# Sharing a group's scores between VectorE and GpSimd, and the order of halvings, folds and row sums in it

## The chip, the cores and the metric

The kernel runs on one core of a Trainium2 chip. The metric is the time of one execution in device microseconds; lower is better. A core has TensorE (PE in the profile), VectorE (DVE), ScalarE (ACT), GpSimd (POOL) and SyncE (SP), each with an in-order queue of instructions of its own, and DMA queues that SyncE and GpSimd issue to.

## The reference

The input x is 8 batches of 512 tokens of 256 numbers. Four blocks follow each other, each adding its result to x: attention A, a feed-forward block, attention B, the same feed-forward block.

```python
x = x + attn_a(layernorm(x))
x = x + ffn(layernorm(x))
x = x + attn_b(layernorm(x))
x = x + ffn(layernorm(x))
# attn_a: 16 heads of 64 channels; it attends over the channels of one token
scores = einsum('bshq,bshk->bshqk', Q / 8, K)     # one 64 x 64 matrix per token and head
w = softmax(where(k > q, -inf, scores))
attn = einsum('bshqk,bshk->bshq', w, V) @ Wo + bo
# ffn
h = silu(x @ w1) * (x @ w2)      # 1024 hidden; w1, w2, h1, h2, w3 ternary with scales
h = gelu(h @ h1); h = gelu(h @ h2); return h @ w3
# attn_b: ordinary causal attention over the 512 tokens, 16 heads of 16
```

Attention A has no matrix product in its middle: each token has its own 64 x 64 causal matrix of products q[i] k[j] for each head, whose exponentials are summed, and summed once more weighted with v[j].

## The kernel before, in words

**Attention A** works in groups: 128 tokens on the partitions and 4 heads, so 8 batches x 4 head groups x 4 token tiles = 128 groups. A causal triangle of 64 is cut into squares: for n = 32, 16, 8, 4, 2, 1 there are 64 / (2n) squares of n x n for a head, and the diagonal is kept by itself. A group's squares make four *units*: unit 0 the 32-squares of two heads, unit 1 all 16-squares, unit 2 the 32-squares of the other two heads, unit 3 all the small ones (8, 4, 2, 1). Units 0, 1 and 2 each have a work tile of 4096 numbers a partition, made in two pieces of 1024: one half of each block of columns for the exponentials (the denominator), the other for the exponentials times v (the numerator). Tiles of units 0 and 2 share a ring of three buffers, unit 1 has one buffer ("w16"), unit 3 one ("ws").

Each unit passes through these operations:

- `scores` (L784): products of q and k, two pieces. Units 0 and 2 on GpSimd, units 1 and 3 on VectorE.
- `exps` (L798): the exponential, on ScalarE.
- `weigh` (L808): times v, on VectorE.
- `halve` (L814): an accumulating DMA, issued from GpSimd's queue, adds one half of the tile to the other (1,024 KB).
- `fold` (L819), units 0 and 2 alone: a further halving, an addition on GpSimd.
- `gather` (L845): VectorE sums the rows of what is left; a row sum for each square size goes into a small tile `red`.
- `add_rows` (L852): GpSimd adds the row sums to `acc`, which holds numerator and denominator of the group. `small_squares` does so for n = 2 and 1 (one addition at L835, two at L852).
- `invert` (L856, VectorE's reciprocal) and `divide` (L860, GpSimd) finish the group; then TensorE turns it over and multiplies with Wo.

**The order is written out by hand.** `AttentionA.step(n)` emits, for step n, the operations of several units at different stages (a software pipeline): the scores of unit n, the exponentials of unit n - 1, weigh and halve of unit n - 2, and so on; four steps make a group. A step has three parts, with a `yield` after each. The instruction queue of each engine holds its instructions in just the order in which `step` emits them, so an instruction that has to wait holds up all that stands behind it on that engine.

**The other blocks** (feed-forward, attention B, feed-forward of the batch before) are a second generator, `after_a`. After each part of a step the driver takes from it as much as is due: every `yield` of `after_a` gives a cost in us, their sum over a batch is `total` (309.5), and this sum is spread evenly over the 64 steps of a batch. The blocks of batch b start 11 steps after the last step of attention A of that batch, so attention A of batch 0 runs by itself and the blocks of batch 7 run by themselves at the end. Work in these blocks is put off with `later` and emitted at the next `flush`.

**The gate of a feed-forward block**: h = silu(p1) * p2 is kept as a high part in a rounded 32-bit format for TensorE and the remainder h - high (L1036, GpSimd), so that two products give the precision of one. The tiles p1 and p2 (128 x 512 each) come from a ring of five PSUM buffers, `ps_f`.

**At the start**, `fit_qkv` prepares the attention weights of one head group (on VectorE for group 0, on GpSimd for groups 1 to 3, with two DMA loads of bias rows and two stores to DRAM on SyncE's queue), and the generator `later_weights` (`prep`) prepares those of the other blocks. `measure` takes mean and variance of a batch's tokens.

Of the kernel before, what the change touches and what calls it, by code (L numbers as in the profile page):

```python
# [26 lines left out]
GW = GH * C  # L27
NG = HID // GW
# [256 lines left out]
def fast_path(ctx: ExitStack, tc: tile.TileContext, k, t, flag):  # L285

    nc = tc.nc
# [182 lines left out]
    def plus(ps, xi):  # L470

        nc.tensor.matmul(ps, ident, xi, start=False, stop=True)

    rends = const.tile([P, 2, NB], F32, name="rends")
    means = const.tile([P, NB, 2, NT], F32, name="means")

# [127 lines left out]
    class AttentionA:  # L604
# [32 lines left out]

        def step(self, n):

            weighed = self.at(n - 2)  # L640
            if weighed[0] is not None:
                self.weigh(*weighed)
            unit = self.at(n)
            on_pool = unit[3] in (0, 2)
            if on_pool:
                half = self.scores(*unit)
                next(half)
            if weighed[0] is not None:
                self.halve(*weighed)
            if on_pool:  # L650
                next(half, None)
            b, i, g, u = self.at(n + 40)
            if u == 0 and g == 0 and i == 0 and b > 0:
                self.x[b] = load_x(b)
            b, i, g, u = self.at(n + 10)
            if u == 0 and g == 0 and i == 0:
                self.measure(b)
            b, i, g, u = self.at(n + 8)
            if u == 0 and g == 0:
                self.live["xn"] = normed(self.x[b][:, i, :], *self.rn[b, i], "a")  # L660
            b, i, g, u = self.at(n - 5)
            if u == NU - 1:
                self.invert(b, i, g)
            b, i, g, u = self.at(n - 4)
            if u == 1:
                self.gather(b, i, g, u)
            b, i, g, u = self.at(n + 7)
            if u == 0 and g == 0:
                nc.scalar.copy(self.live[b, i], self.live.pop("ps_ln"))
            if self.at(n - 1)[0] is not None:  # L670
                self.exps(*self.at(n - 1))
            yield
            if unit[0] is not None and not on_pool:
                for _ in self.scores(*unit):
                    pass
            for args in self.sums:
                self.add_rows(*args)
            self.sums = []
            b, i, g, u = self.at(n - 5)
            if u == NU - 1:  # L680
                self.divide(b, i, g)
            b, i, g, u = self.at(n - 2)
            if u == NU - 1:
                self.small_squares(b, i, g)

            b, i, g, u = self.at(n - 4)
            if u == 0:
                self.fold(b, i, g, u)
            b, i, g, u = self.at(n - 3)
            if u == 2:  # L690
                self.fold(b, i, g, u)
            b, i, g, u = self.at(n - 9)
            if u == NU - 1:
                self.new_x(b, i, g)
            b, i, g, u = self.at(n + 2)
            if u == 0:
                self.keep_qk(b, i, g)
            b, i, g, u = self.at(n - 7)
            if u == NU - 1:
                self.turn_group(b, i, g)  # L700
            b, i, g, u = self.at(n - 8)
            if u == NU - 1:
                self.project_out(b, i, g)
            b, i, g, u = self.at(n + 3)
            if u == 0:
                self.project(b, i, g)
            yield
            b, i, g, u = self.at(n - 4)
            if u == 2:
                self.gather(b, i, g, u)  # L710
            b, i, g, u = self.at(n - 5)
            if u == 0:
                self.gather(b, i, g, u)
            b, i, g, u = self.at(n - 3)
            if u == NU - 1:
                self.gather(b, i, g, u)
            b, i, g, u = self.at(n - 7)
            if u == NU - 1:
                nc.scalar.copy(self.live["att"], self.live.pop("pta"))
            b, i, g, u = self.at(n + 8)  # L720
# [44 lines left out]
        def scores(self, b, i, g, n_u):  # L765

            qv, kt = self.live[b, i, g][:2]
            if n_u == 0:
                acc = ap_.tile([P, 2, GW], F32, tag="acc", name=f"acc_{b}_{i}_{g}", bufs=3)
                self.live[b, i, g].append(acc)  # L770
                nc.vector.tensor_tensor(acc[:, 0, :], qv[:, 0], kt[:, 0], ALU.mult)

            if n_u in (0, 2):
                w = wt.tile([P, 4096], F32, tag="w", name=f"w_{b}_{i}_{g}_{n_u}", bufs=3)
            elif n_u == 1:
                w = wt.tile([P, 4096], F32, tag="w16", name=f"w16_{b}_{i}_{g}")
            else:
                w = wt.tile([P, 2 * SMALL], F32, tag="ws", name=f"ws_{b}_{i}_{g}")
            self.live[b, i, g, n_u] = w
            eng, q = (nc.gpsimd, kt[:, 1]) if n_u in (0, 2) else (nc.vector, qv[:, 0])  # L780
            for n, off, nsq, cols in squares(units[n_u]):
                for e, ev, rows, columns in pieces(w, n, off, nsq, cols):
                    shape = list(e.shape)
                    eng.tensor_tensor(  # L784
                        e, rows(q).to_broadcast(shape), columns(kt[:, 0]).to_broadcast(shape), ALU.mult
                    )
                    yield
# [50 lines left out]
        def gather(self, b, i, g, n_u):  # L838


            w = self.live.pop((b, i, g, n_u))
            for n, off, nsq, cols in squares(units[n_u]):
                if n > 2:
                    red = ap_.tile([P, 2, nsq * n], F32, tag=f"red{nsq * n}", name=f"red_{b}_{i}_{g}_{n_u}_{n}", bufs=2 + (n < 32))
                    nc.vector.tensor_reduce(red, self.columns_of(w, n, off, nsq), AX.X, ALU.add)  # L845
                    self.sums.append((b, i, g, n, cols, red))

        def add_rows(self, b, i, g, n, cols, part):

# [45 lines left out]
    def later(fn):  # L895
        pending.append(fn)

    def flush():
        fns = pending[:]
        pending.clear()  # L900
        for fn in fns:
            fn()
# [111 lines left out]
    def ffn(u, b, xt, nx, after):  # L1014
# [11 lines left out]
        def gate(m, p1, p2, h):  # L1026
            x = silus[:, m % 4]
            nc.scalar.activation(x, p1, AF.Silu, scale=s_sb[:, 0, m : m + 1])  # L1028

            def times():  # L1030
                nc.vector.scalar_tensor_tensor(x, p2, s_sb[:, 1, m : m + 1], x, ALU.mult, ALU.mult)
                later(high)

            def high():
                nc.scalar.copy(h(0, m), x)
                later(lambda: nc.gpsimd.tensor_tensor(h(1, m), x, h(0, m), ALU.subtract))  # L1036

            later(times)

        for m0 in range(0, MC, 2):  # L1040
# [30 lines left out]
            for m in (m0, m0 + 1):  # L1071
                p = ps[m - m0] or [ps_f.tile([P, S], F32, tag="pf", name=f"pw{j}_{u}_{m}") for j in range(2)]
                for j in range(2):
                    products(p[j], m, j, last if ps[0] else slice(0, S))
                flush()
                later(lambda m=m, p=p, h=h: gate(m, *p, h))
                yield 0.5 if ps[0] else 1.8
        for _ in range(2):
            flush()
            yield 1  # L1080

# [254 lines left out]


    each = NT * NG * NU
    total = 309.5
    ET = mybir.EngineType  # L1340
    with tc.manual_schedule(engines={ET.PE, ET.DVE, ET.Activation, ET.Pool}):
        a = AttentionA()
        prep = later_weights()
        fit_qkv(0)
        weights = None
        done, spent = after_a(), 0
        for n in range(-10, a.steps):
            for part, _ in enumerate(a.step(n)):
                if n >= 2:
                    next(prep, None)  # L1350
                while 3 * spent * each < total * (3 * (n - each - 11) + part + 1):
                    spent += next(done)
            if 0 <= n < NG - 1:
                fit_qkv(n + 1)
        for _ in done:
            pass
    judge()
# [86 lines left out]
```

## Time and profile before

| what | value |
|---|---|
| time, median of 3 runs | 4010.42 us (4006.96 to 4017.54) |
| the profiled execution: its own time, its span | 4009.55 us, 4007.6 us |
| busy: PE, DVE, ACT, POOL | 2958.0, 3376.7, 2337.2, 3098.1 us |
| L784 on POOL, 128x1024, 512 of them | 2102 ns each |
| L784 on DVE, 128x1024 of unit 1, 256 of them | 1219 ns each |
| L819 fold, 256 of them | 2512 ns each |
| L814 halving, 384 of them | 878 ns on POOL's queue, 7.7 us to landing (median) |
| L852 row sums, 896 of them in three forms | 701 to 797 ns each |
| L1036 remainder, 128 of them | 1448 ns each |

A row of a timeline gives start, length, engine, line, the operation with output and input, and in brackets the idle time of the engine before it and what ended it. Lengths overlap a little, since an engine begins an instruction while the one before drains; so the cost of an instruction in a full queue is the distance from its start to the next start. "issue" means that the profile names no releaser.

### The profile page before, as it was taken

The numbers are of one execution on the slowest core, as the hardware profiler recorded it, in microseconds if no ns is written. First come the engines' busy times: TensorE is split into PE (matmuls) and PEld (weight loads), VectorE is DVE, ScalarE is ACT, GpSimd is POOL, SyncE is SP. The second block draws the span as 40 slices with busy tenths as digits, with TensorE's granted clock in tenths as the row PEclk, the third lists the DMA queues.
The fourth block names the chain that finished last, engine by engine and source line by source line (L and its number), as shares of the span: only waits on it lengthen the run. The fifth ranks groups of instructions, "written<-read, shape, count | busy, mean of one in ns | idle before, by whom it ended". The sixth has DMA issues, their size and how long they took to land.

```text
span 4007.6 us, 37678 instructions
## 1 busy us (share of the span) xinstructions
PE 2958.0 (74%) x12328; PEld 2012.2 (50%) x12328; DVE 3376.7 (84%) x3777; ACT 2337.2 (58%) x3145; POOL 3098.1 (77%) x3051
## 2 busy tenths in 40 slices
PE   1543478777876888768787788768787778768988
PEld 0311145355653656346553566346653556436847
DVE  4899988998889888998989988998889988897115
ACT  2433465666755766666755767567656667555342
POOL 6688888887888887887888888888888878886211
PEclk7555689888987989889897889879898899879999
DMA  8566777668776777668776688668877687767304
GB/s 240 114 141 145 146 182 182 147 161 199 199 162 126 195 188 196 150 147 210 174 192 139 168 198 214 147 131 198 195 181 151 154 199 205 155 133 210 126 29 167
DMA packets 118653, 671.07 MB, mean 167 GB/s; under 512 B 12704, under 2 KB 31915, under 8 KB 43824
## 3 DMA queue, kind: packets, MB, share of 16 engines
q0 software_dynamic: 78336, 570.46, 62.9%
q1 hardware_dynamic: 40112, 98.11, 6.8%
q8 instruction: 100, 1.64, 0.2%
q14 instruction: 105, 0.86, 0.1%
HBM read 255.90 MB, written 9.96 MB: 66 GB/s over the span
## 4 chain that ended last, share of the span: by engine, by line
DVE 38%; PE 16%; POOL 14%; DMA 12%; issue 8%; ACT 8%; POOLq 0%; DVEq 0%; ACTq 0%
DVE red L845 15%; DMA w<-w 12%; DVE w L808 10%; PE ph L1120 5%; ACT w L798 3%; POOL w L819 3%; DVE ws L808 3%; POOL w L784 3%; PE pqkb L1167 3%; DVE ws L784 3%; POOL acc L852 3%; DVE w L784 2%; POOL w L814 2%; DVE acc L856 2%; POOL h L1036 2%
## 5 line engine op out<-in xcount | busy, mean ns | idle before, releaser
L798 ACT ACTIVATE w<-w 128x2048 f32<-128x2048 f32 x384 | 734.2, 1913 | 653.8 <-POOL w L784 440.8
L1120 PE MATMUL ph<-h,hidden 128*128 128x512 f32 x4096 | 1047.9, 412 | 77.4 <-POOL h L1036 45.5
L784 POOL TENSOR_TENSOR w<-k 128x1024 f32<-128x1024 f32 x512 | 1076.2, 2102 | 9.6 <-ACT k L762 9.0
L1120 PEld LDWEIGHTS ph<-h,hidden 128*128 128x128 f32 x4096 | 795.3, 196 | 282.1 <-POOL h L1036 55.9
L808 DVE TENSOR_TENSOR w<-w,qv 128x1024 f32<-128x1024 f32 x768 | 899.8, 1213 | 22.4 <-ACT w L798 22.3
L845 DVE TENSOR_REDUCE red<-w 128x128 f32<-128x1024 f32 (+1 forms) x384 | 601.8, 1567 | 171.6 <-DMA w<-w 94.6
L819 POOL TENSOR_TENSOR w<-w 128x1024 f32<-128x1024 f32 x256 | 643.1, 2512 | 72.5 <-DMA w<-w 71.9
L814 POOL DMA_DIRECT2D w<-w x384 | 337.1, 878 | 339.7 <-issue 134.8
L852 POOL TENSOR_TENSOR acc<-acc,red 128x256 f32<-128x256 f32 (+1 forms) x640 | 471.0, 736 | 152.3 <-DVE red L845 124.5
L845 DVE TENSOR_REDUCE red<-ws 128x256 f32<-128x2048 f32 (+1 forms) x256 | 435.5, 1743 | 0.0
L746 PE MATMUL qv<-wqv,xnta 128*128 128x512 f32 x512 | 299.3, 715 | 89.9 <-DVE ws L808 82.4
L808 DVE TENSOR_TENSOR ws<-ws,qv 128x1024 f32<-128x1024 f32 (+3 forms) x512 | 294.7, 638 | 49.4 <-ACT ws L798 49.4
L1052 PE MATMUL pw<-xnt,gate 128*128 128x512 f32 (+2 forms) x1152 | 298.8, 419 | 24.9 <-ACT silu L1028 18.0
L784 DVE TENSOR_TENSOR w<-qv,k 128x1024 f32<-128x1024 f32 x256 | 301.3, 1219 | 3.6
L784 DVE TENSOR_TENSOR ws<-qv,k 128x1024 f32<-128x1024 f32 (+3 forms) x512 | 299.8, 648 | 0.0
L868 PE MATMUL bank<-ident,acc 128*128 128x128 f32 x256 | 64.3, 341 | 287.5 <-ACT k L761 287.1
L798 ACT ACTIVATE ws<-ws 128x1920 f32<-128x1920 f32 x128 | 231.5, 1809 | 75.3 <-DVE ws L784 74.7
L1052 PEld LDWEIGHTS pw<-xnt,gate 128*128 128x128 f32 x1152 | 227.6, 213 | 82.1 <-ACT silu L1028 22.3
L1229 ACT ACTIVATE eb<-psb 128x256 f32<-128x256 f32 (+3 forms) x512 | 182.2, 443 | 146.6 <-PE psb L1226 146.3
L1146 PE MATMUL pof<-w,h 128*128 128x256 f32 x1024 | 247.9, 396 | 19.4 <-ACT h L1085 19.4
L1085 ACT ACTIVATE h<-ph,s_sb 128x512 fp32r<-128x512 f32 (+1 forms) x256 | 171.1, 688 | 145.9 <-PE ph L1120 144.6
L856 DVE RECIPROCAL acc<-acc 128x256 f32<-128x256 f32 x128 | 223.2, 1744 | 12.3 <-POOL acc L852 12.3
(143 smaller groups left out, 4723.5 us busy)
## 6 DMA issues: line engine op xcount, KB each, us to landing
w<-w POOLq DMA_DIRECT2D x384, 1024.0 KB, 7.7
hidden<-in_h POOLq DMA_DIRECT2D x128, 1024.0 KB, 7.9
gate<-in_w12p POOLq DMA_DIRECT2D x32, 1024.0 KB, 9.0
w<-w_d SPq DMA_DIRECT2D x16, 1024.0 KB, 12.0
wqv<-wqv_d SPq DMA_DIRECT2D x31, 512.0 KB
wo<-in_wo SPq DMA_DIRECT2D x32, 256.0 KB, 7.4
wbqk<-wbqk_d SPq DMA_DIRECT2D x8, 1024.0 KB
w<-in_h SPq DMA_DIRECT2D x8, 1024.0 KB, 7.0
```

The costliest lines, as they stand in the source:

```text
L746: nc.tensor.matmul(qv.rearrange("p j f -> p (j f)"), xnt[:, c, :], wqv[:, c, :], start=(c == 0), stop=(c == DC - 1),)
L784: eng.tensor_tensor(e, rows(q).to_broadcast(shape), columns(kt[:, 0]).to_broadcast(shape), ALU.mult)
L798: nc.scalar.activation(e, e, AF.Exp, scale=C**-0.5)
L808: nc.vector.tensor_tensor(ev, e, columns(qv[:, 1]).to_broadcast(list(e.shape)), ALU.mult)
L814: nc.gpsimd.dma_start(w[:, :2048], w[:, 2048:], accum_op=ALU.add)
L819: nc.gpsimd.tensor_tensor(w[:, :1024], w[:, :1024], w[:, 1024:2048], ALU.add)
L845: nc.vector.tensor_reduce(red, self.columns_of(w, n, off, nsq), AX.X, ALU.add)
L852: nc.gpsimd.tensor_tensor(rows, rows, part.rearrange("p a (x i) -> p a x i", i=n), ALU.add)
L856: nc.vector.reciprocal(acc[:, 0, :], acc[:, 0, :])
L1052: nc.tensor.matmul(pj[:, toks], w[:, m % 4, j, c, :], xs[:, p, c, toks], start=(p == 0 and c == 0), stop=(p == 1 and c == DC - 1),)
L1120: nc.tensor.matmul(pss[j], w[:, j, c, :], h_in(p, c), start=(p == 0 and c == 0), stop=(p == 1 and c == MC - 1),)
L1146: nc.tensor.matmul(po, h(0, c)[:, i * P : (i + 1) * P], w3[:, c, :], start=(c == 0), stop=False)
```

## The change

- Of the two 16-square score pieces (unit 1), the first moves from VectorE to GpSimd.
- The row sums of units 0 and 2 go into one `red` tile, and one `add_rows` takes both (for 32), after the second of the two is there.
- The order within a step changes: `invert` (now of the unit at n - 6, before n - 5) and the `gather` of unit 1 come first in the step, ahead of `weigh`. The `fold` of unit 0 moves from n - 4 in part 2 to n - 3 in part 1, before the scores; the `gather` of unit 0 from n - 5 to n - 4, that of unit 2 from n - 4 to n - 5; `divide` from n - 5 to n - 6.
- The gate's remainder: TensorE forms x - high in a third PSUM tile (`rest`) from the ring of five, with an identity and a negative identity as weights, and ScalarE copies it out. The step has one more stage, with `flush` after each product instead of after each pair.
- The costs that `after_a` yields for the gate are larger, and `total` becomes 328.9.
- At the start `measure(0)` comes before the first weights, `prep` advances once a step instead of three times, and `fit_qkv` of groups 1, 2, 3 follows steps 4, 14 and 24 instead of 0, 1 and 2.

```diff
+    minus = const.tile([P, P], F32R, name="minus")
+    nc.scalar.activation(minus, ident, AF.Copy, scale=-1.0)
...
         def step(self, n):
+            b, i, g, u = self.at(n - 6)
+            if u == NU - 1:
+                self.invert(b, i, g)
+            b, i, g, u = self.at(n - 4)
+            if u == 1:
+                self.gather(b, i, g, u)
             weighed = self.at(n - 2)
             if weighed[0] is not None:
                 self.weigh(*weighed)
+            b, i, g, u = self.at(n - 3)
+            if u == 0:
+                self.fold(b, i, g, u)
...
             if u == 0 and g == 0 and i == 0:
-                self.measure(b)
+                if b > 0:
+                    self.measure(b)
...
-            b, i, g, u = self.at(n - 5)
-            if u == NU - 1:
-                self.invert(b, i, g)
-            b, i, g, u = self.at(n - 4)
-            if u == 1:
-                self.gather(b, i, g, u)
...
-            b, i, g, u = self.at(n - 5)
-            if u == NU - 1:
-                self.divide(b, i, g)
...
-            b, i, g, u = self.at(n - 4)
-            if u == 0:
-                self.fold(b, i, g, u)
             b, i, g, u = self.at(n - 3)
             if u == 2:
                 self.fold(b, i, g, u)
+            b, i, g, u = self.at(n - 6)
+            if u == NU - 1:
+                self.divide(b, i, g)
...
             b, i, g, u = self.at(n - 4)
-            if u == 2:
+            if u == 0:
                 self.gather(b, i, g, u)
             b, i, g, u = self.at(n - 5)
-            if u == 0:
+            if u == 2:
                 self.gather(b, i, g, u)
...
-            eng, q = (nc.gpsimd, kt[:, 1]) if n_u in (0, 2) else (nc.vector, qv[:, 0])
             for n, off, nsq, cols in squares(units[n_u]):
-                for e, ev, rows, columns in pieces(w, n, off, nsq, cols):
+                for p, (e, ev, rows, columns) in enumerate(pieces(w, n, off, nsq, cols)):
+                    on_pool = n == 32 or n == 16 and p == 0
+                    eng, q = (nc.gpsimd, kt[:, 1]) if on_pool else (nc.vector, qv[:, 0])
...
-                    red = ap_.tile([P, 2, nsq * n], F32, ...)
-                    nc.vector.tensor_reduce(red, self.columns_of(w, n, off, nsq), AX.X, ALU.add)
-                    self.sums.append((b, i, g, n, cols, red))
+                    if n_u != 2:
+                        self.live["red", n] = ap_.tile([P, 2, GW // 2], F32, ...)
+                    red = self.live["red", n]
+                    part = red[:, :, cols.start // 2 : cols.stop // 2]
+                    nc.vector.tensor_reduce(part, self.columns_of(w, n, off, nsq), AX.X, ALU.add)
+                    if n_u != 0:
+                        self.sums.append((b, i, g, n, slice(0, GW), red))
...
-                later(lambda: nc.gpsimd.tensor_tensor(h(1, m), x, h(0, m), ALU.subtract))
+                later(low)
+            def low():
+                rest = ps_f.tile([P, S], F32, tag="pf", name=f"rest_{u}_{m}")
+                nc.tensor.matmul(rest, ident, x, start=True, stop=False)
+                nc.tensor.matmul(rest, minus, h(0, m), start=False, stop=True)
+                later(lambda: nc.scalar.copy(h(1, m), rest))
...
-                flush()
+                    flush()
                 later(lambda m=m, p=p, h=h: gate(m, *p, h))
-                yield 0.5 if ps[0] else 1.8
-        for _ in range(2):
+                yield 1.5 if ps[0] else 2.9
+        for _ in range(3):
...
-    total = 309.5
+    total = 328.9
...
+        a.measure(0)
         fit_qkv(0)
...
-                if n >= 2:
+                if n >= 3 and part == 2:
                     next(prep, None)
...
-            if 0 <= n < NG - 1:
-                fit_qkv(n + 1)
+            if n in (4, 14, 24):
+                fit_qkv(n // 10 + 1)
```

More of the change, by code (lines that the diff above doesn't have):

```diff
@@ L843, in gather @@
                 if n > 2:
-                    red = ap_.tile([P, 2, nsq * n], F32, tag=f"red{nsq * n}", name=f"red_{b}_{i}_{g}_{n_u}_{n}", bufs=2 + (n < 32))
-                    nc.vector.tensor_reduce(red, self.columns_of(w, n, off, nsq), AX.X, ALU.add)
-                    self.sums.append((b, i, g, n, cols, red))
+                    if n_u != 2:
+                        self.live["red", n] = ap_.tile(
+                            [P, 2, GW // 2], F32, tag=f"red{n // 32}", name=f"red{n}_{b}_{i}_{g}"
+                        )
+                    red = self.live["red", n]
[3 more added lines that the diff above has]
+                        self.sums.append((b, i, g, n, slice(0, GW), red))
         def add_rows(self, b, i, g, n, cols, part):
```

## The prediction

> **What bounds the kernel now.** I read the busy time by stretches first, then the queues of VectorE (DVE) and GpSimd (POOL) side by side in one undisturbed stretch, then the waits.
>
> Busy time by stretches (columns: stretch, its length, then busy us and instructions of PE, PE weight loads, DVE, ACT, POOL; then granted clock, DMA share, GB/s):
>
> ```profile
> 300.00:400.00 100.00, 37.65 (x64) 17.93 (x64) 99.73 (x108) 39.00 (x38) 85.25 (x78) 0.50 0.71 147
> ...
> 2100.00:2500.00 400.00, 313.67 (x1345) 218.46 (x1346) 363.55 (x409) 267.45 (x351) 332.20 (x321) 0.88 0.75 180
> ...
> 3800.00:3900.00 100.00, 90.10 (x521) 50.24 (x519) 7.05 (x24) 40.42 (x101) 9.40 (x27) 1.00 0.08 27
> ```
>
> Three stages. Until about 523 us attention A runs alone and DVE is full. From 523 to 3690 us it shares the core with the blocks of the batch before, and DVE (91%) and POOL (83%) are both near full. After 3690 us only TensorE works.
>
> One group of the first stage (POOL's timeline: start, length, engine, line, then in brackets the idle time before it):
>
> ```profile
> 319.12 1.96 POOL L784 TENSOR_TENSOR w<-k 128x1024 f32<-128x1024 f32 x1
> 321.02 0.87 POOL L814 DMA_DIRECT2D w<-w  x1
> 321.63 2.25 POOL L784 TENSOR_TENSOR w<-k 128x1024 f32<-128x1024 f32 x1
> 323.55 0.73 POOL L852 TENSOR_TENSOR acc<-acc,red 128x128 f32<-128x128 f32 x1
> 326.93 0.87 POOL L814 DMA_DIRECT2D w<-w  x1 [2.65 <-issue]
> 327.54 2.35 POOL L852 TENSOR_TENSOR acc<-acc,red 128x128 f32<-128x128 f32 x3
> 329.86 1.95 POOL L784 TENSOR_TENSOR w<-k 128x1024 f32<-128x1024 f32 x1
> 331.75 0.85 POOL L814 DMA_DIRECT2D w<-w  x1
> 332.36 2.23 POOL L784 TENSOR_TENSOR w<-k 128x1024 f32<-128x1024 f32 x1
> 334.28 0.98 POOL L860 TENSOR_TENSOR acc<-acc 128x256 f32<-128x256 f32 x1
> 334.96 2.60 POOL L819 TENSOR_TENSOR w<-w 128x1024 f32<-128x1024 f32 x1
> ...
> 342.83 1.96 POOL L784 TENSOR_TENSOR w<-k 128x1024 f32<-128x1024 f32 x1
> ```
>
> The group repeats after 342.83 - 319.12 = 23.7 us. POOL idles once, 2.65 us, ahead of the second halving (L814); 21.05 us is work. DVE has no gap at all: its 23.7 us is pure work. Note the distance from the first halving (321.02) to the fold (L819) of the same tile at 334.96: 14 us lie between.
>
> ```profile
> 331.17 1.74 DVE L856 RECIPROCAL acc<-acc 128x256 f32<-128x256 f32 x1
> 332.83 2.28 DVE L808 TENSOR_TENSOR ws<-ws,qv 128x1024 f32<-128x1024 f32 x4
> 335.03 2.28 DVE L845 TENSOR_REDUCE red<-w 128x256 f32<-128x2048 f32 x1
> 337.34 2.36 DVE L784 TENSOR_TENSOR w<-qv,k 128x1024 f32<-128x1024 f32 x2
> ```
>
> From start to next start the reciprocal takes 1.66 us, the reduction of the 16-squares 2.31 us, a 16-square score 1.14 us.
>
> What the halving's transfer takes (the answer on line L814), from issue to landing:
>
> ```profile
> DMA to landing us min/median/max: 6.9/7.7/16.7
> ```
>
> In the first stage the median is 7.1 us, in 1000 to 3600 us 7.8 us.
>
> **What the Trainium skill says.** "Perfetto Trace Analysis", DMA Instruction — SWDGE (GPSIMD): such an instruction's shown interval ends when its descriptors are written, not when the data has moved. The trace agrees: L814 is busy 0.87 us and lands at 7.7. "DMA: Bandwidth & Descriptors", Anatomy of one DMA — SWDGE (gpsimd) path: about 2.0 us plus bytes/436 GB/s; for 1,024 KB an estimate of 4.4 us. The trace has none below 6.9, so I use the trace. "GPSIMD Engine Reference", 4.1 Engine selection: two-input elementwise work is about 2 times slower than on VectorE; here 2102 ns (L784 POOL) against 1219 (L784 DVE), 1.7 times. "Perfetto Trace Analysis", Optimization Strategy: a gap that repeats can mean too few buffers. Before, POOL's L784 idles 9.6 us in all, so no run shows one there yet.
>
> **The change, part by part.** All per group; there are 128.
>
> 1. *One 16-square score to POOL.* DVE loses 1.14 us and has 22.6 left. POOL gains 1.90 us (start to start of L784 on POOL).
>
> 2. *One row sum for both 32-halves.* POOL runs four of these additions (L852) for five: minus 0.70 us. DVE's reductions keep their sizes: 0. POOL's attention work is then 21.05 + 1.90 - 0.70 = 22.25 us. By work alone both engines would be level, below 23.7.
>
> 3. *The fold of the first 32-unit moved forward.* In POOL's new order the halving of unit 0 is followed by one score piece of unit 2 (1.92 us) and then at once by the fold, which waits for that transfer. So 0.61 (issue) + 1.92 = 2.5 us cover a landing of 7.1: POOL stands still 4.6 us. Nothing behind it can pass: the second halving, two row sums, the next group's scores. In the built order 85 of 128 groups have just that one piece between; 26 have one weight load's issue (0.6 us) besides. This swallows the old 2.65 us wait, since VectorE has weighed unit 1 by then.
>
> 4. *Reciprocal and 16-reduction ahead.* The group's last row sum (32s) now stands on POOL immediately ahead of the new 16-square piece. On VectorE the reciprocal waits for that row sum, and the 16-reduction stands behind the reciprocal. The new POOL piece writes the tile that this reduction reads, and that tile has one buffer. So between these two POOL instructions lie 1.66 + 2.31 us of VectorE and two handovers (an estimate of 0.15 us together: the reciprocal and the weighing above follow each other without any): POOL stands still 4.1 us, however early VectorE is. Queued behind: the row sums, the second fold, the division, the next scores.
>
> Round the loop once: 22.25 + 4.6 + 4.1 = 30.95 us, against 23.7. VectorE's 22.6 us fits inside; its weighings are ready ahead of the three halvings by my count of the same rows (by 4 us or more). ScalarE too.
>
> 5. *Gate remainders.* POOL loses 128 of 1448 ns (L1036 before). ScalarE gains 128 copies of about 0.6 us (583 ns for a 128x512 copy out of PSUM), beside other work. TensorE gains two f32 passes and one f32r product of 512 columns. In the last stage 16 f32 matmuls of 256 columns take 3.62 us and 64 f32r ones of 512 take 14.89, so 2 x 0.45 + 0.23 = 1.13 us each. In the middle TensorE (78% busy) hides it; uncovered it would cost 112 x 1.13 = 127 us. In the last stage it is bare: 16 x 1.13 = 18 us. The third PSUM tile per chunk in the same ring of five: from nothing to about the 20 us that the gate's products wait now (24.9); I take 0, as POOL's longer round gives slack. The new block costs (309.5 to 328.9) change order only: 0.
>
> 6. *Start.* Measuring batch 0 first brings the first scores forward by about 4 us (projection at 22.4 us now waits for the normalised tile, the weights are ready near 18). Preparations spread out: their 27 us on POOL fall half into the two standstills; 8 us (the rest is mostly the three weight fits, which fall in standstills) stay. Later fits issue their SyncE stores later, still tens of us before their readers; bounds 0 to 10 us. The -1 identity is one small ScalarE instruction: 0.
>
> **The sum**, against the profiled execution (span 4007.6 us, time 4009.55; the median of the runs is 4010.42, 0.02% more).
> First stage: 495 us (28 to 523) for 18.75 groups. After: 18.75 x 30.95 = 580, +8, -4: 584, so +89.
> Middle: between 1000 and 3600 us POOL makes 362 score pieces, four a group: 28.7 us a group, and 3167 us are 110 groups. After: 30.95, + 0.7 (landing 7.8 for 7.1), + 0.9 (the other blocks bring POOL 1.85 us a group of small norms and weight issues; half lands in a standstill) = 32.6. (32.6 - 28.7) x 110 = +429.
> Last: +18.
> Together +536: span 4543, time 4545 us.
> Own range of this case: a middle round of 31.6 (no extra) to 34 (landings near the mean of the late ones): 4435 to 4700.
>
> **Rivals.**
> *Faster: the standstills are not there.* If landings and VectorE's two instructions were covered, VectorE would set the pace as now, 1.14 us shorter: -1.14 x 129 = -147, start -30 (of the 50 us lost there), last stage +18: 3851. It decides if the two standstills together stay below 28.7 - 24.1 = 4.6 us in the middle (24.1 = 22.25 + 1.85). For: POOL idles 17% there now. Against: the 6.9 us floor, and the order. Chance 0.08.
> *Only one standstill counts* (the other falls inside it): round 26.6 in the first stage, 28.3 in the middle: +5, -44, +18, to +100 if other waits stay: 3990 to 4110. Against: they are at different places of one in-order queue, so they add. Chance 0.08.
> *Coupling adds more*: TensorE's longer gate and ScalarE's waits for the late POOL scores (L798 waits 440.8 us for them now) delay the other blocks, and the middle round reaches 35: 4545 + 2.4 x 110 = 4810, from 4700 up. Chance 0.08.
> Forecast 0.76.
>
> **Numbers.** Range 4400 to 4770: the forecast's case and most of the coupling case, leaving out the first two rivals. Faster by over 0.3% (about what this measurement can tell from no change) 0.10, within 0.02, slower 0.88.
>
> **What would show it.** Right: folds (L824 after) waiting for DMA some 4.5 us in most groups, half of all folds; POOL's 128x1024 piece (L789) waiting for the VectorE reduction near 4 us a group; a first-stage period near 31 us; DVE below 80% busy; last stage 18 us longer. Wrong: a period near 23 us, or folds that don't wait.

## The result and the profile after

The changed kernel takes 4719.9 us (median of 4 runs, 4718.78 to 4731.63), the kernel before 4008.69 beside it (4 runs, 4004.39 to 4017.54): a ratio of 1.1777, 95% interval 1.175 to 1.1805. The profiled execution took 4718.78 us, its span is 4717.0. The two engines that were nearly full became less full. The busy time by stretches, same columns as before (length, busy us of PE, PE weight loads, DVE, ACT, POOL, granted clock, DMA share, GB/s):

```profile
300.00:400.00 100.00, 26.41 (x48) 12.63 (x48) 68.30 (x71) 28.04 (x28) 74.05 (x60) 0.59 0.57 118
2100.00:2500.00 400.00, 310.19 (x1193) 216.95 (x1195) 298.09 (x327) 251.44 (x316) 286.52 (x264) 0.88 0.69 164
4500.00:4600.00 100.00, 90.21 (x517) 50.25 (x515) 6.66 (x23) 40.39 (x101) 9.12 (x27) 0.98 0.08 27
```

DVE falls from 99.73 to 68.30 in the first stage and from 363.55 to 298.09 in the middle, while POOL falls too, from 85.25 to 74.05 and from 332.20 to 286.52. Neither is held by its own work any more: both wait. One group on POOL's timeline (start, length, engine, line, in brackets the idle time before and its releaser) shows where:

```profile
373.04 1.95 POOL L789 TENSOR_TENSOR w<-k 128x1024 f32<-128x1024 f32 x1 [4.01 <-DVE red L855]
...
382.84 0.84 POOL L819 DMA_DIRECT2D w<-w  x1
383.45 2.22 POOL L789 TENSOR_TENSOR w<-k 128x1024 f32<-128x1024 f32 x1
389.85 2.35 POOL L824 TENSOR_TENSOR w<-w 128x1024 f32<-128x1024 f32 x1 [4.18 <-DMA w<-w]
392.14 0.87 POOL L819 DMA_DIRECT2D w<-w  x1
...
398.92 0.99 POOL L863 TENSOR_TENSOR acc<-acc,red 128x256 f32<-128x256 f32 x1
403.93 1.95 POOL L789 TENSOR_TENSOR w<-k 128x1024 f32<-128x1024 f32 x1 [4.01 <-DVE red L855]
```

The round, the time after which the group repeats, is 403.93 - 373.04 = 30.9 us, for 23.7 before. It has two waits that the group of before has not: the fold of unit 0 (L824) behind its own halving's transfer, issued 7.0 us earlier, and the new piece of the squares of 16 (L789). What VectorE does between the last row sum and that piece:

```profile
399.95 1.75 DVE L867 RECIPROCAL acc<-acc 128x256 f32<-128x256 f32 x1 [6.50 <-POOL acc L863]
401.62 2.23 DVE L855 TENSOR_REDUCE red<-w 128x256 f32<-128x2048 f32 x1
```

VectorE itself has stood still for 6.50 us when POOL's row sum (398.92) releases the reciprocal; then POOL waits for reciprocal and reduction. So neither is late by work: each waits for the other in turn.

For comparing the runs below I cut each profiled span at two places: the start of the first `ps_ln` product, where the other blocks begin, and the start of the last division on POOL (L860 before, L871 after), where attention A ends. I take the same 110 middle rounds as the prediction.

| kernel | first stage to, us | middle, us (a round) | last stage, us | median of runs, us | ratio (95%) |
|---|---|---|---|---|---|
| before | 523.1 | 3167.2 (28.8) | 317.3 | 4008.69 | |
| after | 614.1 | 3763.6 (34.2) | 339.3 | 4719.9 | 1.1777 (1.175 to 1.1805) |
| e1, fold later | 565.9 | 3753.7 (34.1) | 341.2 | 4663.5 | 1.1629 (1.1609 to 1.1648) |
| e2, reciprocal later | 582.5 | 3529.5 (32.1) | 341.3 | 4457.33 | 1.1116 (1.1097 to 1.1134) |
| e3, both | 561.2 | 3610.4 (32.8) | 338.0 | 4513.63 | 1.1256 (1.1237 to 1.1276) |
| e4, gate back on POOL | 614.9 | 3737.2 (34.0) | 320.3 | 4675.35 | 1.1654 (1.1633 to 1.1676) |
| e6, 16s back on DVE | 609.8 | 3732.0 (33.9) | 339.2 | 4685.58 | 1.1685 (1.1666 to 1.1705) |
| e7, three moves | 528.9 | 3372.6 (30.7) | 339.4 | 4232.1 | 1.0548 (1.0531 to 1.0566) |
| e8, e7 and gate on POOL | 528.1 | 3340.3 (30.4) | 320.7 | 4190.43 | 1.0446 (1.0429 to 1.0464) |
| e9, before + gate | 521.7 | 3228.0 (29.3) | 336.4 | 4085.22 | 1.018 (1.0159 to 1.0202) |
| e10, before + sharing | 550.0 | 3296.1 (30.0) | 318.9 | 4167.26 | 1.0391 (1.0373 to 1.041) |
| e11, e10 + merged sum | 553.9 | 3288.0 (29.9) | 318.6 | 4162.76 | 1.0379 (1.036 to 1.0399) |
| e12, e9 with old costs | 521.3 | 3206.1 (29.1) | 353.0 | 4090.28 | 1.0204 (1.0184 to 1.0224) |
| e13, e11 + fold moved | 541.4 | 3337.0 (30.3) | 317.7 | 4193.7 | 1.0464 (1.045 to 1.0479) |

Of the 709 us between the two spans 91 lie in the first stage, 596 in the middle and 22 in the last.

### The profile page after: what moved, and what is told of

Same layout as the page of the kernel before. It is cut to its first block, busy times and chain, and to the rows that moved or that the text cites. A ratio compares the mean times of both kernels' runs of the same rounds, so it can differ in the third digit from the quotient of the medians.

```text
span 4717.0 us, 38941 instructions
## 1 busy us (share of the span) xinstructions
PE 3197.0 (68%) x12712; PEld 2106.8 (45%) x12712; DVE 3244.7 (69%) x3649; ACT 2465.2 (52%) x3318; POOL 3150.9 (67%) x2923
## 4 chain that ended last, share of the span: by engine, by line
POOL 39%; DVE 20%; issue 17%; PE 14%; ACT 7%; DMA 2%; POOLq 0%; SPq 0%; DVEq 0%; ACTq 0%
POOL w L789 17%; DVE red L855 8%; POOL w L824 7%; POOL acc L863 6%; POOL w L819 5%; PE ph L1137 4%; DVE w L813 4%; DVE ws L813 3%; PE qv L749 2%; PE pw L1069 2%; DVE ws L789 2%; ACT w L803 1%; DMA w<-w 1%; POOL acc L871 1%; PE pyb L1251 1%
## 5 line engine op out<-in xcount | busy, mean ns | idle before, releaser
L789 POOL TENSOR_TENSOR w<-k 128x1024 f32<-128x1024 f32 x640 | 1325.0, 2071 | 531.8 <-DVE red L855 510.9
L803 ACT ACTIVATE w<-w 128x2048 f32<-128x2048 f32 x384 | 734.9, 1914 | 745.3 <-POOL w L789 440.1
L1137 PE MATMUL ph<-h,hidden 128*128 128x512 f32 x4096 | 1031.6, 409 | 6.6 <-DMA hidden<-in_h 6.6
L749 PE MATMUL qv<-wqv,xnta 128*128 128x512 f32 x512 | 433.5, 996 | 877.2 <-DVE ws L813 787.0
L824 POOL TENSOR_TENSOR w<-w 128x1024 f32<-128x1024 f32 x256 | 607.5, 2373 | 551.9 <-DMA w<-w 510.9
L749 PEld LDWEIGHTS qv<-wqv,xnta 128*128 128x128 f32 x512 | 139.1, 299 | 1048.4 <-issue 655.6
L863 POOL TENSOR_TENSOR acc<-acc,red 128x256 f32<-128x256 f32 x512 | 438.9, 857 | 16.3 <-DVE red L855 6.2
L819 POOL DMA_DIRECT2D w<-w x384 | 336.8, 877 | 89.6 <-DVE acc L774 32.3
L1069 PE MATMUL pw<-xnt,gate 128*128 128x512 f32 (+2 forms) x1152 | 315.3, 427 | 16.6 <-DVE xnt L994 6.4
L789 DVE TENSOR_TENSOR ws<-qv,k 128x1024 f32<-128x1024 f32 (+3 forms) x512 | 299.8, 648 | 0.0
L1163 PEld LDWEIGHTS pof<-w,h 128*128 128x128 f32 x1024 | 202.0, 198 | 41.3 <-issue 12.9
```

Of the source, the lines that this page charges most:

```text
L749: nc.tensor.matmul(qv.rearrange("p j f -> p (j f)"), xnt[:, c, :], wqv[:, c, :], start=(c == 0), stop=(c == DC - 1),)
L789: eng.tensor_tensor(e, rows(q).to_broadcast(shape), columns(kt[:, 0]).to_broadcast(shape), ALU.mult)
L803: nc.scalar.activation(e, e, AF.Exp, scale=C**-0.5)
L819: nc.gpsimd.dma_start(w[:, :2048], w[:, 2048:], accum_op=ALU.add)
L824: nc.gpsimd.tensor_tensor(w[:, :1024], w[:, :1024], w[:, 1024:2048], ALU.add)
L863: nc.gpsimd.tensor_tensor(rows, rows, part.rearrange("p a (x i) -> p a x i", i=n), ALU.add)
```

## The experiments

The first theory was the prediction's: two standstills, one behind the other in POOL's queue, each of which can be taken away by moving its step. The rivals were that one hides in the other, and that the coupling with the other blocks does the damage.

### e1_fold_late: the fold of unit 0 one step later

The line that goes stood ahead of the scores of its step; the new one stands behind the scores of the next.

```diff
-            b, i, g, u = self.at(n - 3)
-            if u == 0:
-                self.fold(b, i, g, u)
...
+            b, i, g, u = self.at(n - 4)
+            if u == 0:
+                self.fold(b, i, g, u)
```

> Changed kernel with one edit: the fold of unit 0 waits one step longer (behind the scores of the next group's unit 0), so that about 9 us of GpSimd work cover its transfer. Theory (two GpSimd standstills, one after the other in one queue, set the round): the 4.15 us wait for the DMA goes, the 4.0 us wait for VectorE stays; first-stage period 30.86 to about 26.5, time 4150 to 4250. Rival 'only one standstill counts': no change (4700), the other wait grows by as much. Rival 'GpSimd's added work is the bound': period stays near 30, time over 4600.

Measured: 4663.5 us, far above. Here are the new piece on POOL's timeline and, from VectorE's, the reduction of unit 0:

```profile
407.20 1.95 POOL L789 TENSOR_TENSOR w<-k 128x1024 f32<-128x1024 f32 x1 [4.47 <-DVE red L855]
```

```profile
402.10 1.22 DVE L855 TENSOR_REDUCE red<-w 128x128 f32<-128x1024 f32 x1 [5.40 <-POOL w L824]
```

The fold no longer waits. But unit 0's reduction still stands at the head of VectorE's queue, ahead of reciprocal and reduction of the 16s, and now it waits 5.40 us for the later fold; POOL's piece then waits for all three. The round is 28.0 us (379.24 to 407.20): one loop through both queues took the place of the wait that was removed. The first stage gains 48 us by it, the middle only 10: from 1200 to 3500 us POOL's halvings (L819) wait 238.3 us in e1 and 48.3 in the changed kernel.

### e2_inv_after: the reciprocal behind the score of the 16s

The line that goes stood at the head of the step.

```diff
-            b, i, g, u = self.at(n - 6)
-            if u == NU - 1:
-                self.invert(b, i, g)
...
                 for _ in self.scores(*unit):
                     pass
+            b, i, g, u = self.at(n - 6)
+            if u == NU - 1:
+                self.invert(b, i, g)
```

> Changed kernel with one edit: the reciprocal goes behind the weighing and the 16-square score in VectorE's order, so that the reduction that frees the 16-square tile no longer stands behind it. Theory: the 4.0 us wait for VectorE goes, the 4.15 us wait for the DMA stays; period about 26.5, time 4150 to 4250. Rival 'only one standstill counts': no change, the DMA wait is what matters and E1 takes all. Rival 'added GpSimd work': over 4600.

Measured: 4457.33 us; the direction is right, the gain 262 us and not the 470 or more expected. The two waits of the changed kernel again, in e2, on POOL's timeline:

```profile
372.82 2.36 POOL L824 TENSOR_TENSOR w<-w 128x1024 f32<-128x1024 f32 x1 [4.19 <-DMA w<-w]
...
384.60 1.95 POOL L789 TENSOR_TENSOR w<-k 128x1024 f32<-128x1024 f32 x1 [1.70 <-DVE red L855]
```

and, a round earlier, the reduction of the 16s on VectorE's:

```profile
353.63 2.29 DVE L855 TENSOR_REDUCE red<-w 128x256 f32<-128x2048 f32 x1 [5.73 <-DMA w<-w]
```

The wait at the piece falls from 4.0 to 1.7 us, not to nothing: the reduction of the 16s, free of the reciprocal, waits for the halving of the same tile, which POOL could issue only when the waiting fold was through. The two standstills are not independent; one feeds the other.

### e3_both: both moves

> Both edits. Theory: both standstills gone, VectorE (22.6 us of work a group) sets the pace; first-stage period 22.6 to 23, middle round 27.6 to 28.5, time 3800 to 3950, faster than the kernel before. Rival 'the gate by TensorE and ScalarE slows the middle': first-stage period near 23 but the middle round still over 30, time over 4100. Rival 'added GpSimd work is the bound': not below 4200.

Measured: 4513.63 us, slower than e2. In the first stage the round is 28.0 us, as in e1, because the reduction of unit 0 waits for the late fold; that is still shorter than e2's 28.5. The loss lies in the middle, 81 us longer than e2's: from 1200 to 3500 us VectorE's reductions wait 361.5 us for folds (30.4 in e2), and POOL's halvings wait 271.8 us, for VectorE mostly (52.1 in e2). That was the lesson: the theory of two separate standstills is wrong as a recipe, though it priced the changed kernel's round rightly. The next kernel opens the loop seen in e1 too.

### e7_three and e8_three_gate_pool: three moves, and the gate taken back

e7 is e3 with the reduction of unit 0 one step later:

```diff
-            b, i, g, u = self.at(n - 4)
-            if u == 0:
-                self.gather(b, i, g, u)
             b, i, g, u = self.at(n - 5)
-            if u == 2:
+            if u in (0, 2):
                 self.gather(b, i, g, u)
```

> The changed kernel with three steps moved: unit 0's fold one step later, behind that step's scores on GpSimd; the reciprocal behind the score of the squares of 16 of its step; and the reduction of unit 0 one step later, behind unit 2's halving, so that it does not head VectorE's queue before its fold is made. Theory that the round is held by three overlapping loops of waits and by nothing else: with all three opened, GpSimd's own work of 22.25 us holds the first stage's round again, at 22.6 to 23.5 us; the middle round comes to about 28 us, and the whole to 3850 to 3950 us, below the kernel before. Rival, that GpSimd's attention steps also wait on VectorE's other work and on the gate's new chain in the middle: the first stage reaches 22.6 to 23.5 us, but the middle round stays above 30 us, and the whole above 4100 us.

> The run before this with the gate's remainder back on GpSimd, with the old costs and flushes. Theory that the gate's chain over TensorE and ScalarE costs in the last stage alone: 20 us less in the last stage, the middle within 10 us of the run before this, so about 20 to 30 us less in all. Rival, that GpSimd is the bound of the middle once the standstills are gone, so that 1.35 us a group come back there: the middle is some 110 to 150 us longer, and the whole longer by 90 to 130 us.

Measured: 4232.1 and 4190.43 us. The three moves take 488 us off the changed kernel, and its first stage comes back to 528.9 us. But the round there is 25.6 us on average (from one division to the next, four rounds), not 22.6 to 23.5, and the middle's is 30.7, as the rival said. In e8 the gate on POOL gives 18.7 us in the last stage and 32 in the middle, more than the theory allowed. Some 10 of these 32 may be chance: the profiled execution of e7 (4243.0 us) is the longest of its four, and by the medians e8 is 41.7 us faster in all. What POOL's 1.35 us a group may cost there is less than what the gate's new way cost; the two cannot be told apart.

### e6_no16: the changed order, the 16s wholly on VectorE

```diff
-                    on_pool = n == 32 or n == 16 and p == 0
+                    on_pool = n == 32
```

> The changed kernel with both pieces of the score of the squares of 16 on VectorE, all else as changed. Theory that the reductions' place in the order makes the standstill, and not who makes the piece: GpSimd's round in the first stage is 20.35 us of work, the fold's wait of 4.15 and about 4 at the first piece of the squares of 32 or at the sum, 28 to 29 us, and the whole 4450 to 4500 us. Rival, that the sharing of the one 16 tile makes it: the wait is gone, the round about 24.6 us, and the whole 3950 to 4050 us.

Measured: 4685.58 us, 34 us below the changed kernel. Without the shared piece the same wait stands in front of the next instruction that needs the reduction, the row sum:

```profile
371.55 0.73 POOL L863 TENSOR_TENSOR acc<-acc,red 128x256 f32<-128x256 f32 x1 [4.08 <-DVE red L855]
373.60 0.61 POOL L840 TENSOR_TENSOR ws<-ws 128x256 f32<-128x256 f32 x1 [1.32 <-DVE ws L813]
...
387.82 2.37 POOL L824 TENSOR_TENSOR w<-w 128x1024 f32<-128x1024 f32 x1 [4.19 <-DMA w<-w]
```

4.08 for 4.01 us, and 4.19 at the fold; the round is 30.4 us. So this order makes the standstill even without the sharing and without the single buffer of the 16 tile. (The Trainium skill, "Perfetto Trace Analysis", Optimization Strategy, says that a repeating gap can mean too few buffers; in this trace it repeats in every group, and e6 shows that it stays when no one on POOL wants the buffer. No run gave the tile a second one.) It came out slower than I expected because the small squares (L840) add 1.32 us: in the changed kernel VectorE had weighed them while POOL made the piece, and no wait shows there.

### e10, e11, e13: the sharing in the old order

e10 is the kernel before with `on_pool` as in the change; e11 adds the merged row sum.

> The kernel before with one part of the change alone: the first piece of the score of the squares of 16 on GpSimd, in the old order. Theory that the order costs and the sharing does not: between the row sum that the reciprocal waits for and GpSimd's new piece the old order has 7 us of GpSimd work (two pieces, the division, a fold), against 6.3 us of VectorE's (reciprocal, weighing of the small squares, reduction of the squares of 16), so no standstill of 4 us appears; first stage's round 23 to 24 us, the middle about level, the whole 3900 to 4080 us. Rival, that the single tile of the squares of 16 makes the two engines wait for each other wherever the piece stands: a wait of 2 us or more ahead of that piece in most groups, round over 25 us, the whole over 4150 us.

> The run before this with the merged row sum of the squares of 32 as well, the order still the old one. By work VectorE has 22.6 us a group and GpSimd 22.25. Theory as before: 0.7 us of GpSimd less, first stage's round 22.7 to 23.7 us, the whole 10 to 80 us below the run before this, 3850 to 4000 us. Rival, that the sum of both halves comes later and with it the reciprocal, so that a wait takes the 0.7 us back: the whole within 10 us of the run before this, or above.

Measured: 4167.26 and 4162.76 us, both slower than before. The times fall where the rivals put them, with rounds of 25.2 and 25.5 us for 23.7. But e10's rival named the wrong place: in the first stage there is no wait at the new piece in an ordinary group. In e10, first POOL, then VectorE:

```profile
343.95 0.87 POOL L815 DMA_DIRECT2D w<-w  x1 [2.29 <-DVE w L809]
```

```profile
336.61 1.22 DVE L846 TENSOR_REDUCE red<-w 128x128 f32<-128x1024 f32 x1 [2.52 <-POOL w L820]
```

The new piece stands ahead of unit 2's fold on POOL and puts it off by 1.9 us; VectorE, now lighter, reaches that unit's reduction early and waits 2.52 us for the fold; its weighing of unit 1, behind it, is late by so much, and POOL's halving waits 2.29 us for that. Taking 1.14 us off VectorE gained nothing in this stage, since VectorE was moved from working to waiting.

In the middle POOL does wait at the new piece. Its waits for VectorE's reduction from 1200 to 3500 us, before and then e10 (line that waited, releaser, us in total, times, longest):

```profile
POOL acc L852 <- DVE red L845: 70.9, 38, 4.2
```

```profile
POOL w L785 <- DVE red L846: 83.7, 38, 5.9
```

But this is nearly the wait of before, moved from the row sum of the 16s (L852) to the piece that now stands ahead of it. What grew in the middle is POOL's work: 25.9 us of a round of 30.0 in e10, 24.0 of 28.8 before. Of the piece's 1.9 us only some 0.7 went into waits that were there already.

e13 puts the fold directly behind the piece; its old place, behind the small squares, goes:

```diff
                 for _ in self.scores(*unit):
                     pass
+            b, i, g, u = self.at(n - 3)
+            if u == 2:
+                self.fold(b, i, g, u)
             for args in self.sums:
                 self.add_rows(*args)
```

> The kernel before with the sharing and the merged row sum in the old order, and one step moved: unit 2's fold stands directly behind GpSimd's new piece, ahead of the row sum and the small squares. Theory: the 25.5 us of the run with sharing and merged sum is a loop (fold of unit 2, VectorE's reduction of it, reduction of the small squares, weighing of unit 1, halving, three row sums, two pieces, division, fold of unit 0, new piece, row sum, small squares, back to the fold); with the fold 3.3 us further ahead the loop is 22.2 us, below VectorE's own 22.6. First stage's round 22.6 to 23.2 us, VectorE's 2.8 us wait ahead of the reduction and GpSimd's 2.7 us ahead of the halving gone; middle round 27.3 to 28.3 for 28.8; the whole 3850 to 3970 us, below the kernel before. Rival: the other blocks' work falls into the loop in the middle and uses up its 0.4 us of slack, so the middle is level or longer and the whole 4000 to 4080 us, though the first stage is shorter.

Measured: 4193.7 us, a miss in the whole and half a miss in the stage: the round falls to 24.3 to 25.1 us, and there it stops. On POOL:

```profile
362.26 1.02 POOL L815 DMA_DIRECT2D w<-w  x1
...
367.50 0.85 POOL L815 DMA_DIRECT2D w<-w  x1
...
374.07 1.95 POOL L785 TENSOR_TENSOR w<-k 128x1024 f32<-128x1024 f32 x1 [0.74 <-DVE red L849]
376.74 2.37 POOL L820 TENSOR_TENSOR w<-w 128x1024 f32<-128x1024 f32 x1 [0.71 <-DMA w<-w]
```

The fold waits for the halving issued at 367.50, so its transfer took some 9.2 us. The waits that went let the three halvings of a group be issued closer together, and the median landing between 300 and 500 us is 9.1 us for 7.0 before. I had counted the loop through the engines and not the one through the DMA. The middle became 49 us longer than e11's; from 1200 to 3500 us the new piece waits 131.3 us for VectorE's reduction there, and 61.8 in e11. A shorter round in the quiet stage was no shorter in the crowded one.

### e4, e9, e12: the gate

e4 is the changed kernel with the remainder, its costs and flushes as before; e9 the kernel before with the gate's part alone; e12 is e9 with the old yields of the products and the old `total`; the third `flush` behind them, with its yield of 1, stays.

> Changed kernel with the gate's remainders back on GpSimd (with the costs and flushes that belong to it), all else kept. Theory: first stage unchanged (period 30.9), last stage about 20 us shorter (318), the middle round longer by 0.7 to 1.35 us since GpSimd has that work again: 4770 to 4850 in all. Rival 'TensorE's longer gate explains the 1.4 us by which the middle round exceeds the forecast (34.0 against 32.6)': the middle round falls to about 32.6 or below, time under 4600.

> The kernel before with the gate's part of the change alone: the remainder by two products on TensorE and a copy on ScalarE, with the changed costs, flushes and yields. Theory that it costs in the last stage alone: the first stage as before, the middle within 15 us, the last stage 18 to 21 us longer, the whole 4010 to 4045 us. Rival, that GpSimd bounds the middle of the kernel before and gains its 1.35 us a group there: the middle is 100 to 150 us shorter, and the whole 3880 to 3930 us.

> The kernel before with the gate's remainder by TensorE and ScalarE, but with the old costs of the blocks (yields and total), so that the other blocks' work is emitted beside the same steps of attention as before. Theory that the extra 60 us in the middle of the gate-only kernel come from the changed spread of the blocks over the steps: the middle is within 15 us of the kernel before, the last stage 19 us longer, the whole 4020 to 4045 us. Rival, that they come from the work itself (TensorE's products, the third tile in the ring of five, ScalarE's copies in ScalarE's queue): the middle stays 40 us or more longer, the whole 4065 to 4100 us.

Measured: 4675.35, 4085.22 and 4090.28 us. e4 was expected to be slower than the changed kernel and is 44 us faster: 19 in the last stage, 26 in the middle. So in the middle the relief of POOL, 1.35 us a group, was worth less than the gate's new way costs; the 26 us are the difference of the two. e9 shows the same on the kernel before: 61 us in the middle, against both its theory (within 15) and its rival (a gain). The table loads of ScalarE at the line of silu, before and then e9 (columns: line, engine, operation, count, then busy us, ns of one, and the engine's idle time before):

```profile
L1028 ACT ACT_TABLE_LOAD x49 | 62.9, 1283 | 0.9
```

```profile
L1030 ACT ACT_TABLE_LOAD x72 | 92.4, 1283 | 1.3
```

Over all lines there are 317 before and 361 in e9, as in the changed kernel: 44 x 1.283 = 56 us of ScalarE. e12, which has the flush after each product too but the old costs, has 315; so it is the changed costs that bring the loads. No price of them shows: as a whole e12 (4082.14 to 4094.84) is not faster than e9 (4076.21 to 4090.16), and it lies where the rival put it. Its middle is 22 us shorter than e9's, still 39 longer than before, and its last stage is 36 us longer than before, for e9's 19. These two belong together: with the third yield the costs of a batch come to 311.5 against a `total` of 309.5, so the blocks fall behind, and what is left at the end runs in the last stage. TensorE is busy 327.8 us there in e12, and 311.2 in e9. So most of e9's 61 us in the middle come from the work itself. Which of TensorE's products, the third tile in the ring of five and ScalarE's copies makes them was not separated.

The parts add up. Above the kernel before that ran beside each, e11 (the sharing with the merged sum) is 151 us and e9 (the gate) 75, together 226; e7, which has both and the three moves, is 222. So the 488 us that the three moves take off are about what these places in the new order cost.

## Why the prediction was right, point by point

The direction, the two standstills and the round of the first stage were right; the time lies 20 us above the forecast's own range and inside that of the rival "coupling adds more", which had 0.08. The stated range, 4400 to 4770, held it because it took in most of that rival. The mechanism that the rival named shows only in part: the gate makes 26 us of the middle (e4), but ScalarE's exponentials wait 440.1 us for POOL's scores, where they waited 440.8 before.

1. *One score to POOL*: 1.91 us from start to start, for 1.90. Right. That it would be harmless by work, "level, below 23.7", was true of the work and no guide to the time: alone it makes the span 157 us longer (e10).
2. *One row sum less*: of no weight: e11 is 4.5 us below e10, with overlapping runs, as its rival said; its first stage is even 4 us longer.
3. *The fold*: 4.18 us for 4.6. The transfer was as priced (7.0 us); the piece between issue and fold takes 2.22 us there and not 1.92, so 2.8 us are covered and not 2.5.
4. *Reciprocal and reduction ahead of the piece*: 4.01 for 4.1. The reason named, one buffer of the tile, is one way by which it bites; e6 shows that the order is enough. The round: 30.9 for 30.95. First stage: +91 for +89.
5. *The gate*: last stage +22 for +18. In the middle the prediction had 0, with TensorE at 78% busy to hide it; the runs have 26 us (e4, from the changed kernel) to 61 (e9, from before). That hiding is what failed. (The last stage is not TensorE's alone, as the prediction read its line: ScalarE is busy 40.42 of 100 us there. At 90.10 TensorE still sets its length.) "The new block costs change order only: 0" did not: they bring 44 table loads, but e12 without these is no faster than e9.
6. *The start*: the first score on POOL comes at 24.3 us for 28.0, so -3.7 for -4. Right; the 8 us of preparations were not measured by themselves.
7. *The middle round*, "30.95 + 0.7 (landing) + 0.9 (half of the other blocks' POOL work, the other half in a standstill) = 32.6", is the term that was too small: measured 34.2, and +596 for +429. The whole is 173 us above the forecast, and 167 of them lie here. POOL's waits in the middle, 1200 to 3500 us (line that waited, releaser, us in total, times, longest):

```profile
POOL w L789 <- DVE red L855: 276.1, 77, 5.1
POOL w L824 <- DMA w<-w: 263.3, 58, 6.9
POOL w L819 <- DVE acc L774: 16.7, 11, 2.5
POOL w L824 <- DVE ws L789: 15.1, 4, 5.1
POOL w L819 <- DVE w L813: 12.6, 4, 3.4
POOL w L824 <- DVE w L813: 11.4, 3, 5.9
```

These 2300 us are 67.2 rounds of 34.2. POOL is busy 1644.2 us of them, 24.46 a round, against 22.85 in the first stage (74.05% of 30.86): the other blocks' work is +1.6. It idles 9.76 a round, against 8.0: +1.75. The waits at the pieces (L789) are 4.16 a round and the fold's 4.38, all releasers together: neither is shorter than in the first stage. So no part of the other blocks' work shows as hidden by a standstill, where the prediction hid half of it; and the landing's 0.7 did not appear at the fold as such (4.38 for 4.18). New are waits of the halvings (L819) for VectorE and ScalarE, 0.7 us a round with the small rows of that view, which the first stage lacks. The gate's 26 us, 0.24 a round, are contained in these sums. Work hides in a wait only if it is issued between that wait's two ends; what is put elsewhere lengthens the loop. That last sentence fits these numbers, but no run moved the other blocks' work to test it.

The rival "standstills are not there" fell with the first stage. "Only one counts" fell with the timeline, where both stand in each group; but e1 to e3 show that it held a truth that the forecast missed: removing one of them does not give its whole 4 us back. The faster rival's sum, VectorE's 1.14 us less in every round, fell even where no standstill of 4 us exists (e10, e13).

**What stays open.** e8 has all three loops opened and the old gate, and its middle round is still 1.6 us above that of before (30.4 for 28.8); e10, e11 and e13 are 1.1 to 1.5 above. In e10 the two waits shown account for it in the first stage, and in the middle POOL's account shows more work, not more waiting; for e8 and e13 the waits of the middle were not followed to their ends. Two things were not tried: a second buffer for the 16 tile, and another place for the other blocks' work on POOL. No version that I ran beats the kernel before.

## What to carry to other kernels

When two engines pass work to and fro, price a reordering by loops: follow each wait back through both queues until you return to the instruction, and sum work, handovers and DMA landings round it; the longest loop is the round, and removing it gains only the distance to the next longest (here 30.9, then 28.0 and 28.5 us, then 25.6). Balancing the work of two engines can be worth nothing, or cost time as it did here, if the moved instruction stands ahead of something for which the relieved engine waits. Slack counted in a stage where a pipeline runs alone should not be carried to one where other work is interleaved.

## What the runs showed of the hardware

- A halving of 1,024 KB (an accumulating DMA) that no other halving overlaps mostly lands 6.9 to 7.0 us after its issue in the first stage. One that is issued while the halving ahead is still on its way mostly lands later, by about as much as the two overlap beyond 1.9 us. Overlap and landing: 2.2 us and 7.3 (before), 2.7 and 7.8 (changed kernel), 4.2 and 9.2, 4.5 and 9.4 (e13; e1 has about the same). There are exceptions, up to 11.5 us in e13. So, as an estimate from these figures, about 5.1 of the 7.0 us are spent moving, and two such transfers move one behind the other. The rate agrees: 147 GB/s at a busy share of 0.71 (before, 300 to 400 us) are 207 GB/s while the DMA engines move, and at that rate 1,024 KB take 5.1 us. The 4.4 us that the prediction worked out from the Trainium skill and set aside is still further off when two overlap.
- A load of an activation table takes 1283 ns, the mean at every line that has such loads, 361 in the changed kernel (the Trainium skill, "ScalarE activation tables: per-element evaluation and per-set limits", What a function is on this engine, gives the same figure). How work of several blocks is interleaved sets their number: other costs for the same work made 361 of them in e9, and the old costs 315 in e12.
